# Layer 0 of a two-layer kernel: fourteen products of k with an exponential, made by GpSimd and not by VectorE

## The chip, the cores and the metric

The kernel runs on one core of a Trainium2 chip, as one program with one launch. The metric is the device time of that core in microseconds (us): the median of three runs, and beside it the span of one profiled execution, from its first instruction to its last. In the profile the engines are called PE (TensorE, matrix products and transposes), PEld (its weight loads), DVE (VectorE), ACT (ScalarE), POOL (GpSimd) and SP (SyncE, which issues most of the DMA transfers).

## The reference, cut to what matters

The input x has 4 batches of 512 tokens with 512 channels; fside, called k here, has the same shape and serves as both k and v of the mixing step. Two layers each add to x the result of a mixture of experts, whose input is a token-mixing step (called WKV below). The mixing step of layer 0, for every batch and channel, is:

```python
decay = exp(-exp(w)) * (0.5 + 0.5 * tf)          # one number for each batch and channel
ek = exp(minimum(k, 30));  ekv = ek * k
# two sums with decay over the 512 tokens, forwards (f) and in reverse (b), of ekv and of ek:
#   a = a * decay + ekv[t];   b = b * decay + ek[t]
euk = exp(minimum(u + k, 30))                     # u is the bonus of the channel
num = nf + nb - ekv + euk * k
den = df + db - ek + euk
out = sigmoid(x) * (num / maximum(den, 1e-8)) * (0.8 + 0.2 * tf)
```

`euk` is the exponential that holds the bonus, and `euk * k` is the product that the change is about. `out` is normed, goes to 8 experts (2 for each token) and a shared expert, and is added to x. Layer 1 does the same with its own w and u, and with 32 experts, 6 for each token.

## The kernel before

Channels lie on the 128 partitions and tokens along the free dimension. A unit is one batch and one block of 128 channels, a tile of 128 x 512 in 32 bits; there are NU = 16 of them, numbered n = 4 b + c. Layer 0 works through them in one loop `for n in range(NU)`, followed by routing, a table of slots that is written and read back through DRAM, and the experts (`routed`). Layer 1's WKV (`wkv1`, from line 1043 on) runs on VectorE beside layer 0's experts, and then come layer 1's shared expert and its 32 experts.

The order of instructions on every engine is the order in which the program writes them (a manual schedule for ScalarE, TensorE, VectorE, GpSimd and SyncE). Each engine works through its own queue in that order, and an instruction waits only for the operands it needs and for the buffers it writes.

For one unit the work of layer 0's WKV is spread as follows.

- `turn(n)`: TensorE transposes k, ScalarE copies it to kA (L435, L436).
- `front(n)`: VectorE makes the two arguments of the exponentials (L448, L450), `v[:, 0, :]` and `euk`. There are three buffers of each.
- `front_exps(n)`: ScalarE makes the two exponentials in place (L457, L458).
- `mid(n)`: VectorE multiplies both by k (L465 for the sums, L466 for `eukv`, which has two buffers) and runs `scans`: two scans from the end (L307), a correction of one column (L310), two scans from the front (L312). The scans write over v.
- `sums(n)`: TensorE adds the scans' results and the bonus terms in PSUM, which turns the four sums into den and num (L475, L476; L476 for num reads `eukv`), and ScalarE makes the reciprocal of den as exp(-ln) (L478 to L480).
- `back(n)`: VectorE corrects the reciprocal and forms the output (L487 to L490).

In iteration n the program writes `sums(n - 1)`, then `front(n + 1)` and `front_exps(n + 1)`, then ScalarE and TensorE work for other units and for the shared expert, then `mid(n)`, and then `back(n - 1)`. So the exponentials of a unit are made one iteration ahead of its products, and its products and scans one iteration ahead of its sums. For iterations with b >= 2, GpSimd writes the slots of an earlier batch to the table between the units (`write_slots`, an indirect DMA for each column, L395): three after `mid(n)` in the first two units of a batch and two in the third. In the first units GpSimd also writes zeros to a buffer (L700) and blanks the tables (L292 to L294).

Later, in layer 0's experts, GpSimd makes a product of its own: `hrow` from `upt` and `sgt` (L977), 128 x 256, two operands in SBUF.

Of the kernel before, what the change touches and what calls it, by code (L numbers as in the profile page):

```python
# [14 lines left out]
ALU = mybir.AluOpType  # L15
# [18 lines left out]
def adaln_ffn_kernel(  # L34
# [26 lines left out]
    nc = tc.nc  # L61
# [241 lines left out]
    def scans(l, b, c, v):  # L303

        dec, _, _, inv = (m[:, c, b : b + 1] for m in decay[l])
        for h in range(2):
            nc.vector.tensor_tensor_scan(  # L307
                v[:, h, ::-1], dec.to_broadcast([P, S]), v[:, h, ::-1], 0.0, ALU.mult, ALU.add
            )
        nc.vector.tensor_scalar(v[:, :, 0], v[:, :, 0], inv, None, ALU.mult)  # L310
        for h in range(2):
            nc.vector.tensor_tensor_scan(v[:, h, :], dec.to_broadcast([P, S]), v[:, h, :], 0.0, ALU.mult, ALU.add)  # L312
# [108 lines left out]
    NU = len(units)  # L421
# [38 lines left out]
    def mid(n):  # L460
        b, c = units[n]
        kT = kA[:, c, b * S : (b + 1) * S]
        v, euk = fronts.pop(n)
        eukv = wk.tile([P, S], F32, tag="eukv", name=f"eukv{n}")
        nc.vector.tensor_tensor(v[:, 1, :], v[:, 0, :], kT, ALU.mult)  # L465
        nc.vector.tensor_tensor(eukv, euk, kT, ALU.mult)  # L466
        scans(0, b, c, v)
        mids[n] = (v[:, 0, :], euk), (v[:, 1, :], eukv)

# [224 lines left out]
    for n in range(NU):  # L694
# [12 lines left out]
        if n == 0:  # L707
            mid(0)
# [44 lines left out]
        if n:  # L753
            mid(n)
# [537 lines left out]
    for h in range(NHALF):  # L1292
# [3 lines left out]
        for b in range(NB):  # L1296
            n = f"{h}_{b}"
# [64 lines left out]
```

## Time and profile before

| | before |
|---|---|
| median of three runs | 1505.91 us (1503.96 to 1506.1) |
| the profiled execution | 1506.29 us |
| its span | 1504.5 us |
| PE busy | 1393.8 us, 93% of the span |
| VectorE busy | 696.1 us, 46% |
| ScalarE busy | 397.6 us, 26% |
| GpSimd busy | 572.3 us, 38% |
| L465, L466 (16 of each) | 11.0 us busy in each group, median 684 and 685 ns |
| L307, L312 up to 190 us | 32 of each (two a unit), about 1.2 us one |

Shares of the whole span hide the stages: layer 0's WKV runs from about 10 to 198 us, layer 0's experts with layer 1's WKV from about 235 to 490 us, and TensorE is full in most of what follows. Busy rows in slices are tenths of a slice of 37.6 us. In a timeline each row has a start and a length in us, the engine, the line, the operation with its operands (written tile, arrow, read tiles), and how many equal instructions are merged in it. Where two are merged the length is that of both.

### The profile page before, as it was taken

What the parts mean: (1) busy time and instruction counts of PE and PEld (TensorE: products, weight loads), DVE (VectorE), ACT (ScalarE), POOL (GpSimd) and SP (SyncE); (2) the same over time, 40 slices, a digit from 0 to 9 for tenths busy, and PEclk for the clock granted to TensorE, in tenths of its full rate; (3) what the DMA queues carried; (4) which work ended last, traced back from release to release, by engine and by line L of the source; (5) the groups of instructions that cost most, each with busy time, mean ns of one, the idle gap of its engine ahead of it and who ended that gap; (6) DMA issues with size and microseconds to landing.
All of it is one profiled execution on the core that took longest, in us unless ns stands there. A gap on an engine that the chain in (4) does not pass through costs nothing. (4 is left out here: it accounts for less than half of the span.)

```text
span 1504.5 us, 16067 instructions
## 1 busy us (share of the span) xinstructions
PE 1393.8 (93%) x4927; PEld 823.6 (55%) x4927; DVE 696.1 (46%) x1260; ACT 397.6 (26%) x962; POOL 572.3 (38%) x564
## 2 busy tenths in 40 slices
PE   5788888988878799999999999999999999999997
PEld 3355456766556454444445655555555565555654
DVE  7899958999991259411112222222222222222221
ACT  5667643544443251000001111111111111111110
POOL 1001235665564100545543343434344344333332
PEclk9899999999999999999999999999999999999999
DMA  8121216554454742010136554667446586546442
GB/s 301 67 77 57 78 50 182 89 119 102 94 145 91 241 149 72 1 58 29 48 109 192 132 163 115 165 155 208 105 110 187 143 230 166 139 131 164 109 95 42
DMA packets 118188, 184.71 MB, mean 123 GB/s; under 512 B 19864, under 2 KB 64940, under 8 KB 118040
## 3 DMA queue, kind: packets, MB, share of 16 engines
q1 hardware_dynamic: 82216, 125.28, 24.6%
q0 software_dynamic: 35296, 56.63, 20.4%
q8 instruction: 66, 1.08, 0.3%
q10 hardware_dynamic: 528, 1.05, 0.2%
q14 instruction: 82, 0.67, 0.1%
HBM read 151.02 MB, written 52.64 MB: 135 GB/s over the span
## 5 line engine op out<-in xcount | busy, mean ns | idle before, releaser
L941 PE MATMUL pout<-w,hT 128*128 128x512 f32 (+1 forms) x432 | 201.1, 598 | 1.3 <-DVE hT L934 0.8
L946 POOL DMA_INDIRECT out_dram<-kA,put x52 | 83.0, 1596 | 279.3 <-DVE kA L945 146.2
L900 POOL DMA_INDIRECT acc<-z1d,put x119 | 123.3, 1036 | 123.0 <-PE pza L913 65.2
L982 DVE SCALAR_TENSOR_TENSOR hrow<-pup,tab,sgt 128x352 f32<-128x352 f32 x84 | 49.1, 584 | 249.4 <-issue 128.9
L395 POOL DMA_INDIRECT table<-pay,r1sloti x96 | 95.0, 989 | 172.7 <-ACT sg L1304 111.9
L945 DVE COPY kA<-pout 128x512 f32<-128x512 f32 x84 | 58.1, 692 | 176.0 <-PE pout L941 164.0
L966 PE MATMUL pgate<-w,kA 128*128 128x352 f32 x416 | 132.8, 462 | 6.1 <-PEq L1027 6.0
L970 PE MATMUL pup<-w,kA 128*128 128x352 f32 x416 | 131.6, 459 | 0.0
L941 PEld LDWEIGHTS pout<-w,hT 128*128 128x128 f32 (+1 forms) x432 | 76.8, 192 | 68.1 <-issue 54.1
L981 ACT ACTIVATE sgt<-pgate 128x352 f32<-128x352 f32 x84 | 38.9, 463 | 250.6 <-PE pgate L966 225.8
L966 PEld LDWEIGHTS pgate<-w,kA 128*128 128x128 f32 x416 | 75.3, 190 | 49.9 <-issue 16.6
L913 PEld LDWEIGHTS pza<-ident,acc 128*128 128x128 f32 x584 | 72.0, 141 | 51.9 <-issue 33.1
L970 PEld LDWEIGHTS pup<-w,kA 128*128 128x128 f32 x416 | 77.4, 190 | 39.7 <-issue 0.2
L913 PE MATMUL pza<-ident,acc 128*128 128x128 f32 x584 | 87.1, 274 | 11.3 <-DMA acc<-z0d,put 9.4
L395 POOL DMA_INDIRECT table<-r0pay,r0sloti x32 | 35.0, 1093 | 160.3 <-DVE r0sloti L386 112.1
L923 ACT COPY kA<-pza 128x256 f32<-128x256 f32 x103 | 38.3, 372 | 205.6 <-DVE kA L922 159.8
L900 POOL DMA_INDIRECT acc<-z0d,put x51 | 66.0, 1294 | 58.2 <-ACT zgT L917 40.2
L941 PE MATMUL pout<-zT,hT 128*128 128x512 f32 (+1 forms) x192 | 87.8, 593 | 0.0
L1148 PE MATMUL g<-zT,w 128*128 128x512 f32 (+1 forms) x192 | 86.5, 593 | 0.0
L1148 PE MATMUL u<-zT,w 128*128 128x512 f32 (+1 forms) x192 | 86.3, 592 | 0.0
L1313 PE MATMUL o<-w,kA 128*128 128x512 f32 (+1 forms) x192 | 84.5, 593 | 0.0
L966 PE MATMUL pgate<-zT,kA 128*128 128x352 f32 x256 | 81.3, 460 | 1.9 <-PEq L1027 1.9
(301 smaller groups left out, 2219.0 us busy)
## 6 DMA issues: line engine op xcount, KB each, us to landing
w<-in_L_ffn_w_dram SPq DMA_DIRECT2D x44, 704.0 KB
zT<-in_L_ffn_w_dram SPq DMA_DIRECT2D x20, 704.0 KB
w<-in_L_ffn_w_dram SPq DMA_DIRECT2D x22, 512.0 KB
zT<-in_L_ffn_w_dram SPq DMA_DIRECT2D x10, 512.0 KB
w<-in_L_ffn_w_dram SPq DMA_DIRECT2D x22, 192.0 KB
acc<-in_x_dram SPq DMA_DIRECT2D x4, 1024.0 KB
xa<-acc SPq DMA_DIRECT2D x4, 1024.0 KB
z0d<-zr SPq DMA_DIRECT2D x16, 256.0 KB
```

The lines of the kernel that those rows point to most:

```text
L395: ins = nc.gpsimd.indirect_dma_start(out=table, out_offset=bass.IndirectOffsetOnAxis(ap=sloti[:, t, j : j + 1], axis=0), in_=pay[:, t, j, ...
L900: nc.gpsimd.indirect_dma_start(out=rows(e, s), out_offset=None, in_=zd, in_offset=bass.IndirectOffsetOnAxis(ap=put_at[:, e * NS + s : e * ...
L913: nc.tensor.transpose(pza[which][:, c * P : (c + 1) * P], rows(e, s)[:, c * P : (c + 1) * P], ident)
L941: nc.tensor.matmul(po, hT[:m, j, :], dv[:m, j, :], start=(j == 0), stop=(j == nf - 1))
L945: nc.vector.tensor_copy(row, po)
L946: nc.gpsimd.indirect_dma_start(out=outs(n), out_offset=bass.IndirectOffsetOnAxis(ap=at, axis=0), in_=row, in_offset=None, bounds_check=T - ...
L966: nc.tensor.matmul(pg, zt[:, c, :], gv[:, c, :], start=(c == 0), stop=(c == NC - 1))
L970: nc.tensor.matmul(pu, zt[:, c, :], uv[:, c, :], start=(c == 0), stop=(c == NC - 1))
L981: nc.scalar.activation(sgt, pg, AF.Silu)
L982: nc.vector.scalar_tensor_tensor(hrow, pu, tab[:, col, 1:2], sgt, ALU.mult, ALU.mult)
L1148: nc.tensor.matmul(p[: m + more], wv[:, c, f : f + m + more], zT[:, c, b * S : (b + 1) * S], start=(c == 0), stop=(c == NC - 1),)
L1313: nc.tensor.matmul(po, hid[:m, j, i * P : (i + 1) * P], dv[:m, j, :], start=(j == 0), stop=(j == len(FCH) - 1))
```

## The change

One line of `mid` is changed. For units 1 to 14 the product `eukv = euk * k` is issued to GpSimd, for units 0 and 15 to VectorE as before. Nothing else is edited; on VectorE the scans of a unit now follow L465 directly, and on GpSimd the fourteen products stand among the memsets, the zero and blank writes and the slot writes in the program's order: the product of unit 1 after the three L700, that of unit 2 after both blanked tables, those of units 9 and 10 and of 13 and 14 behind three slot writes each.

```diff
         v, euk = fronts.pop(n)
         eukv = wk.tile([P, S], F32, tag="eukv", name=f"eukv{n}")
         nc.vector.tensor_tensor(v[:, 1, :], v[:, 0, :], kT, ALU.mult)
-        nc.vector.tensor_tensor(eukv, euk, kT, ALU.mult)
+        (nc.gpsimd if 0 < n < NU - 1 else nc.vector).tensor_tensor(eukv, euk, kT, ALU.mult)
         scans(0, b, c, v)
         mids[n] = (v[:, 0, :], euk), (v[:, 1, :], eukv)
```

## The prediction

> **What bounds the kernel now.** First the span in 40 slices of 37.6 us, to see which engine is full where this code runs (the first five slices):
>
> ```profile
> PE   5788888988878799999999999999999999999997
> DVE  7899958999991259411112222222222222222221
> ```
>
> VectorE is at 8 to 9 tenths there, TensorE at 5 to 8. Next the table of windows, which cuts layer 0's sixteen units into stretches (window and its length, then busy us and count for PE, PEld, DVE, ACT and POOL, granted clock, DMA share, GB/s):
>
> ```profile
> 11.00:50.00 39.00, 24.13 (x77) 13.35 (x78) 33.72 (x59) 27.60 (x52) 4.19 (x9) 0.87 0.75 269
> 50.00:95.00 45.00, 38.34 (x134) 22.08 (x135) 43.45 (x73) 26.79 (x50) 0.00 (x0) 0.89 0.29 94
> 95.00:140.00 45.00, 39.96 (x155) 23.18 (x155) 43.25 (x95) 31.65 (x59) 9.41 (x8) 0.99 0.18 65
> 140.00:187.00 47.00, 40.34 (x140) 22.62 (x139) 44.18 (x129) 31.79 (x58) 9.43 (x8) 0.97 0.17 62
> ```
>
> From 50 to 187 us VectorE is busy 130.9 of 137 us, and the rest is the step from one instruction to the next. GpSimd is nearly empty. Third, VectorE's own waits up to 235 us, to see where it is not the bound:
>
> ```profile
> DVE ssq_parts L819 <- ACT sq L791: 5.2, 1, 5.2
> ...
> DVE ratio L274 <- ACT lom L252: 3.5, 1, 3.5
> ...
> DVE zT L490 <- ACT zT L498: 1.0, 1, 1.0
> ```
>
> In the timeline the 3.45 us wait ends at 44.36 us and the 0.97 us wait at 28.81; the 5.2 us wait lies behind the last unit, at 201 us. So up to 44.4 us ScalarE sets the pace (it runs without a gap from 36.6 to 44.3), and from 44.4 to 198 us VectorE does. After that a chain of logits, routing, table writes (to 229 us) and the first gather (235 us) hangs on VectorE's last unit, and TensorE fills nearly all the rest. What VectorE wins or loses between 44.4 and 198 us therefore moves everything behind it, one for one; the chain of waits at the end of the span shows only the last expert and says nothing of this stage.
>
> **What is removed.** Fourteen of the sixteen L466 products leave VectorE. One unit as it runs now (start, length, engine, line):
>
> ```profile
> 54.31 0.68 DVE L465 TENSOR_TENSOR v<-v,kA 128x512 f32<-128x512 f32 x1
> 54.91 0.68 DVE L466 TENSOR_TENSOR eukv<-euk,kA 128x512 f32<-128x512 f32 x1
> ...
> 55.52 2.33 DVE L307 TENSOR_TENSOR_SCAN v<-dec,v 128x512 f32<-128x512 f32 x2
> ...
> 56.20 0.61 ACT L458 ACTIVATE euk<-euk 128x512 f32<-128x512 f32 x1
> ```
>
> One product lasts 0.68 us but holds its queue from 54.91 to 55.52, 0.61 us, since the next instruction starts under its tail. Units 1 and 2 (L466 at 20.17 and 30.76 us) lie before 44.36 us: their time only lengthens the 3.45 us wait, so they win nothing. Units 3 to 14 win 12 x 0.605 = 7.3 us.
>
> **What is added, and when.** GpSimd has nothing queued that holds a product up for long, so it starts one as soon as ScalarE has made that unit's euk. The ACT line above is already the euk of unit 5, one unit ahead: it ends at 56.81 us, inside unit 4's scans. The ends of L458 for units 6, 7, 8, 11 and 12 fall likewise (65.74, 77.05, 87.77, 126.23, 135.74 us), beside the scan pairs of the unit before; that of unit 4 (44.22) meets L465 of unit 3. Units 9 and 13 sit behind three table writes each (to about 113 and 161 us), and fall on their own first scans; units 10 and 14 sit behind three more and fall on the four instructions of `back`. The product is wanted late (TensorE's L476 of unit 13 is at 169.69 us, 7 us after that product would end), and its buffer is free in time, so I cost lateness at nothing: the cover is the 6 (unit 2) to 16 us (unit 5) between a product's end and its L476. Table writes behind a product move 1.3 us; the table is read only at 231 us. Product 3 (at 36.7 us) and those before it may cost up to the 3.45 us wait for free. That leaves products 4 to 14, eleven.
>
> **What one costs.** The trace has the same operation at half the size: layer 0's experts multiply hrow on GpSimd while VectorE runs layer 1's scans. Its row, and two places where it meets VectorE:
>
> ```profile
> L977 POOL TENSOR_TENSOR hrow<-upt,sgt x35: 726/742/1737, 247.4 to 490.4; 128x256 f32<-128x256 f32 x35
> ```
>
> ```profile
> 336.09 1.56 DVE L1054 TENSOR_TENSOR zT<-zT,kA 128x512 f32<-128x512 f32 x1
> ...
> 336.36 0.73 POOL L977 TENSOR_TENSOR hrow<-upt,sgt 128x256 f32<-128x256 f32 x1
> ```
>
> ```profile
> 316.01 3.38 DVE L307 TENSOR_TENSOR_SCAN v<-dec,v 128x512 f32<-128x512 f32 x2
> 316.71 1.60 POOL L977 TENSOR_TENSOR hrow<-upt,sgt 128x256 f32<-128x256 f32 x1
> ```
>
> L1054 takes 0.69 us undisturbed, here 1.56; two scans take 2.33, here 3.38; and the GpSimd product itself stretches from 0.73 to 1.60. The two engines take turns. I went through all thirty products between 247 and 453 us. The nine that lie under the one-input reciprocal (L1057) leave it at 3.35 us. The other twenty-one cost VectorE 0.29 to 1.05 us each, 12.5 us together, 0.60 on average; the twelve among them at scan pairs average 0.58. A single-input L1051 doubles as well (0.96 for 0.48).
>
> The duration at 512 columns has no row. Bounds from L977: 0.73 us, if all of it were fixed, and 1.48, if none were. The Trainium skill, GPSIMD Engine Reference, section Performance versus the Vector engine, gives 4497 ns for such an operation on 2048 columns; a line through that and the row's 742 at 256 has 2.1 ns a column, so an estimate of 742 + 256 x 2.1 = 1278 ns. The row measures the small end; I take 1.28 and keep 1.48. The 0.54 us that are added hold VectorE in full where it is held at all, so one product costs 0.60 + 0.54 = 1.14 us. Bounds: 0.29 (the added length hides) to 1.05 + 0.74 = 1.79.
>
> A rule to weigh against that: the same skill's page SBUF — State Buffer, section SBUF: two separate sides, says that GpSimd shares one pair of ports with VectorE, that an instruction keeps it to its end, and that only a VectorE instruction with two SBUF inputs or in a two-port mode needs it. By the rule alone each product takes its whole 1.28 us: 11 x 1.28 - 7.3 = +6.8 us. The rows charge less, since an instruction's start-up runs under the other's tail (0.29 at scan ends for a 0.73 us product): 11 x 1.14 - 7.3 = 12.5 - 7.3 = **+5.2 us**. The rows decide.
>
> Against the profiled execution (1506.29 us, its span 1504.5 and 1.8 around it) that gives 1511.5 us; it stands 0.4 above the median of 1505.91, so I predict **1511.1 us**.
>
> **The rivals.** (1) *GpSimd truly runs beside the scans.* The removed time comes through: 1505.9 - 7.3 = 1498.6 us. For it: VectorE is the bound and GpSimd empty. Against: the stretched L307 and L977 above. It would be faster by a measurable amount only if a product cost under (7.3 - 3.0)/11 = 0.39 us; three of the twenty-one did, at half the size. This is the one on the other side. (2) *The loss about cancels the gain:* products 10 and 14 meet L487 and L489, which read one operand from PSUM and may pass freely, and some added length hides. With 0.4 to 0.9 us a product, 4.4 to 9.9 - 7.3: 1503.0 to 1508.5 us. (3) *The dear collision is the rule:* three of six products that start in the first scan of a pair cost 1.0 or so; if all do, 11 x (1.0 + 0.54) - 7.3 = +9.7, or 1515.6 us; at 1.48 us long, 1517.8. (4) *GpSimd's queue is late* and L476 waits: it needs over 6 us of delay behind table writes that take 1.0 to 1.9 us each, three at a time; no time of its own. That nothing is moved is excluded: the built program has fourteen L466 on GpSimd and two on VectorE.
>
> **How the numbers follow.** About 0.2% (3 us) can be told from no change. Forecast 0.60 (1509 to 1514), rival 3 0.12, rival 2 0.19, rival 1 0.08, the rest 0.01. Slower by over 3 us: 0.60 + 0.12 = 0.72. Within: 0.19 + 0.01 = 0.20. Faster: 0.08. The range leaves out rival 1, the bottom of rival 2 and the rare top: 1503.5 to 1517.5.
>
> **What would show it.** VectorE's L466 count falls from 16 to 2, and a POOL row for L466 x14 appears, above 1.28 us on average because it waits. L307 and L312 before 190 us show lengths of 1.7 us or more where all are about 1.2 now. The time from L465 of unit 3 to L465 of unit 15 (44.66 and 186.66 us now, 142.0 us) grows by about 5 us, and later stages keep their length. If that distance shrinks, the scans are not held, and I am wrong; if it grows and the total doesn't, the stage was not what moves the rest; if POOL's L466 last 1.28 us with scans untouched, rival 1 holds.

## The result and the profile after

The changed kernel takes 1512.64 us (median of 9 runs, 1511.32 to 1514.87) against 1506.10 us (9 runs, 1503.96 to 1510.47). The ratio is 1.0042, with a 95% interval of 1.0032 to 1.0052: slower by 6.3 us, between 4.8 and 7.8. The forecast was 1511.1 us, slower by 5.2.

The profiled execution took 1514.87 us, with a span of 1513.1 us. It is the slowest of the nine, so below its stages are compared and not its total.

First the group of the moved products, with the shortest, median and longest duration in ns:

```profile
L466 POOL TENSOR_TENSOR eukv<-euk,kA x14: 1270/1500/2131, 21.1 to 170.1; 128x512 f32<-128x512 f32 x14
...
L466 DVE TENSOR_TENSOR eukv<-euk,kA x2: 685/685/685, 11.4 to 192.9; 128x512 f32<-128x512 f32 x2
```

Fourteen of sixteen have moved. One lasts 1.27 us where it doesn't wait, and half of them last 1.50 us or more. Next the table of windows, in the stretches that were shown of before:

```profile
50.00:95.00 45.00, 37.93 (x132) 21.50 (x133) 43.52 (x61) 25.96 (x49) 6.96 (x4) 0.89 0.29 94
95.00:140.00 45.00, 40.13 (x148) 22.61 (x146) 43.06 (x94) 29.29 (x56) 14.24 (x12) 0.96 0.18 65
140.00:187.00 47.00, 40.46 (x143) 23.16 (x142) 44.73 (x100) 31.07 (x58) 12.95 (x11) 0.96 0.17 62
```

VectorE (third pair) is busy 131.3 of 137 us, as before (130.9), but it gets less far: 255 instructions in that time and not 297, and the moved products are only eleven of the difference. It is "busy" with instructions that wait inside themselves, and for neither an operand nor a buffer. A wait of this kind shows in no list of waits. It shows in the length of single instructions, as here in unit 4 (timeline of the changed kernel):

```profile
54.45 0.68 DVE L465 TENSOR_TENSOR v<-v,kA 128x512 f32<-128x512 f32 x1
...
55.16 2.34 DVE L307 TENSOR_TENSOR_SCAN v<-dec,v 128x512 f32<-128x512 f32 x2
...
56.68 1.88 POOL L466 TENSOR_TENSOR eukv<-euk,kA 128x512 f32<-128x512 f32 x1 [11.56 <-ACT euk L458]
...
57.54 1.04 DVE L310 TENSOR_SCALAR v<-v,inv 128x2 f32<-128x2 f32 x1
```

The product of unit 5 starts as soon as its euk is there, inside the second scan of unit 4. It waits for that scan, runs, and L310, a correction of one column that takes 0.23 us, takes 1.04. The same unit before, with the two scans from the front behind it:

```profile
57.88 0.23 DVE L310 TENSOR_SCALAR v<-v,inv 128x2 f32<-128x2 f32 x1
58.15 2.34 DVE L312 TENSOR_TENSOR_SCAN v<-dec,v 128x512 f32<-128x512 f32 x2
```

The products of units 7 and 9 in the changed kernel:

```profile
77.74 1.27 POOL L466 TENSOR_TENSOR eukv<-euk,kA 128x512 f32<-128x512 f32 x1 [9.18 <-ACT euk L458]
...
77.86 3.35 DVE L312 TENSOR_TENSOR_SCAN v<-dec,v 128x512 f32<-128x512 f32 x2
...
113.36 2.39 DVE L465 TENSOR_TENSOR v<-v,kA 128x512 f32<-128x512 f32 x1
...
113.91 1.27 POOL L466 TENSOR_TENSOR eukv<-euk,kA 128x512 f32<-128x512 f32 x1
```

The pair of scans takes 3.35 us where it took 2.34, and L465 takes 2.39 where it took 0.68. What products 4 to 14 cost VectorE, each read off the stretched instruction against its length before:

| product of unit | VectorE instruction held | us lost |
|---|---|---|
| 4 | L274 (1.24 for 0.17) | 1.07 |
| 5, 6, 8, 12 | L310 (1.04 or 1.05 for 0.23) | 0.81 to 0.82 |
| 7, 10, 11, 14 | the pair L312 (3.35 to 3.37 for 2.34) | 1.02 to 1.03 |
| 9, 13 | L465 (2.39 and 2.40 for 0.68) | 1.71 |

Together they cost 11.85 us, 1.08 on average. VectorE's waits before 245 us have changed in two places that matter:

```profile
DVE t L487 <- ACT r L480: 1.2, 1, 1.2
DVE ratio L274 <- ACT lom L252: 1.0, 1, 1.0
```

The wait at L274, 3.45 us before, has taken up what the first three products cost. The wait at L487 of the last unit was 0.49 us before. The start of a unit's L465 against before tells the rest: unit 3 +0.61 us, unit 9 +1.15, unit 10 +3.44, unit 13 +3.84, unit 14 +6.16, unit 15 +5.69. The table that was read back is converted at 240.2 us, before at 233.7: **+6.5 us**, about what the medians differ by. Its rows, before and after (the start stands behind the durations in ns):

```profile
L850 POOL CAST put<-tab x1: 960/960/960, 233.7 to 233.7; 128x128 int32<-128x128 f32 x1
```

```profile
L850 POOL CAST put<-tab x1: 1206/1206/1206, 240.2 to 240.2; 128x128 int32<-128x128 f32 x1
```

### The profile page after: what moved, and what is told of

Read it like the earlier page. It is cut to its first block, busy times and chain, and to the rows that moved or that the text cites. A ratio compares the mean times of both kernels' runs of the same rounds, so it can differ in the third digit from the quotient of the medians.

```text
span 1513.1 us, 16077 instructions
## 1 busy us (share of the span) xinstructions
PE 1399.0 (92%) x4927; PEld 827.1 (55%) x4927; DVE 702.2 (46%) x1246; ACT 397.2 (26%) x962; POOL 590.0 (39%) x578
## 3 DMA queue, kind: packets, MB, share of 16 engines
q8 instruction: 66, 1.08, 0.3%
q10 hardware_dynamic: 528, 1.05, 0.2%
## 5 line engine op out<-in xcount | busy, mean ns | idle before, releaser
L312 DVE TENSOR_TENSOR_SCAN v<-dec,v 128x512 f32<-128x512 f32 x64 | 80.5, 1300 | 1.1
```

## The experiments

A total of a single run is a weak measure here. Layer 0's experts, from the table to layer 1's first sigmoid, took 287.7 us in the profiled execution of before and 286.2 to 292.4 us in those of kernels that do the same work there. The start of unit 3, where VectorE takes over the pace from ScalarE, varies too: three runs below have it 1.5 to 1.8 us earlier than before, one of them with more work on VectorE. So each run is read first by how the start of a unit's L465 (or the same product under a shifted line number) moves against before from unit 3 to unit 15. By this measure the change stands at +5.08 us. The totals, against runs of the kernel before on the same chip, stand beside it.

**The product left out.**

```diff
-        nc.vector.tensor_tensor(eukv, euk, kT, ALU.mult)
+        if not 0 < n < NU - 1:
+            nc.vector.tensor_tensor(eukv, euk, kT, ALU.mult)
...
-        mids[n] = (v[:, 0, :], euk), (v[:, 1, :], eukv)
+        mids[n] = (v[:, 0, :], euk), (v[:, 1, :], euk if 0 < n < NU - 1 else eukv)
```

> Leaves out the product of units 1 to 14 on every engine (their sums read euk in its place, so num is not the reference's there). Theory (the stage is VectorE's and moves all behind it, and each product gone gives back 0.50 us, as the units without a collision in the changed kernel's trace show): 12 x 0.50 = 6.0 us less, about 1500 us, no L307 or L312 above 1.25 us before 200 us. Rival (another engine takes over as the bound as soon as VectorE is relieved): less than 2 us gained, with new idle time on VectorE between 45 and 190 us.

In the trace every undisturbed unit gains 0.47 to 0.50 us, and from unit 3 to unit 15 the start moves by -5.0 us (from -1.83 to -6.84); the table is converted at 226.9 us, 6.8 earlier. The total is 1508.61 us all the same, ratio 1.0025 (1.0017 to 1.0033). The reason lies in the experiment: with other numbers in num the router chooses other experts, and layer 0 gets 37 tiles of 128 slots where it had 35 (the count of hrow products in the two profiles). So the run shows the size of the gain and that it is passed on as far as the table, and its total says nothing. One wait of 0.72 us appeared, VectorE for ScalarE's sum of squares.

**The product on both engines.** GpSimd writes the buffer first, VectorE after it.

```diff
+        if 0 < n < NU - 1:
+            nc.gpsimd.tensor_tensor(eukv, euk, kT, ALU.mult)
         nc.vector.tensor_tensor(eukv, euk, kT, ALU.mult)
```

> VectorE keeps all sixteen products, and GpSimd makes those of units 1 to 14 too, into the same buffer and ahead of VectorE. Theory (the two engines take turns): the collisions alone, eleven at 1.08 us on average, 11.9 us, so about 1518 us. Rival (the change loses by handing TensorE the product later, or by GpSimd's queue): VectorE hands over as before, so within 2 us of 1506.

1524.99 us, ratio 1.0123 (1.0107 to 1.0139). From unit 3 to unit 15 the start grows from +4.79 to +17.45 us, 12.7 us for ten collisions (that of product 4 falls ahead of unit 3's L465). The 4.8 us before that come for the most part from VectorE's waits for GpSimd's writes of units 1 and 2 (2.3 and 2.9 us), which my design brought in and which I had overlooked. TensorE gets the product from VectorE at its old place, so late handover isn't what costs: the collisions are. In units 9 and 13 they cost 3.5 us each, where the change lost 2.3 net of its gain: L465 again takes 2.39, and the next unit's product now meets the first scan of L312 at its start, which takes 3.04 us for 1.22.

**The product beside `back`.**

```diff
+        if on_pool:
+            hold(nc.gpsimd.tensor_tensor(eukv, euk, kT, ALU.mult), "scan")
```

Here `marks["scan"]` is the last scan of the unit, and `on_pool` is true for units 1 to 14.

> As the change, but GpSimd's product waits for the last scan of its own unit, so that it runs beside the four instructions of back. Theory, if only an instruction with two operands in SBUF has to take turns: L487, which reads den from PSUM, passes, L488 waits about 0.65 us; 12 x (0.65 - 0.50) = 2 us, about 1508 us. If every VectorE instruction has to take turns, each product costs its 1.27 us less little: 12 x (1.2 - 0.5) = 8 us, about 1514 us. Rival (late handover): the product is 3 to 5 us later than in the change, so slower than the change, above 1513 us.

```profile
68.80 0.67 DVE L493 SCALAR_TENSOR_TENSOR t<-den,r 128x512 f32<-128x512 f32 x1
...
69.06 1.28 POOL L473 TENSOR_TENSOR eukv<-euk,kA 128x512 f32<-128x512 f32 x1 [8.58 <-DVE v L312]
...
69.50 1.38 DVE L494 SCALAR_TENSOR_TENSOR t<-t,r 128x512 f32<-128x512 f32 x1
```

L493 (L487 before), which reads den from PSUM, keeps its 0.67 us under the running product. L494, with both operands in SBUF, takes 1.38 for 0.69. Such a unit loses 0.69 and gains 0.49, +0.20 us, and six units show just that. Five show +0.47 to +0.53; they have small routing instructions between the scans and back, and one of these is held (a cast of 32 columns takes 1.14 us for 0.18). From unit 3 to unit 15 the start grows by 3.82 us, where the change has 5.08, with a later handover: in the stage the place decides. The total does not show it: 1512.68 us, ratio 1.0038 (1.0024 to 1.0052), about that of the change and more than the stage accounts for (the table is at +3.3 us). In the profiled execution 1.9 us more came in layer 0's experts, which is inside the spread given above; what holds the median up is open.

**Two halves.** The first 256 columns wait for the last scan, the others for L488.

```diff
+            hold(nc.gpsimd.tensor_tensor(eukv[:, : S // 2], euk[:, : S // 2], kT[:, : S // 2], ALU.mult), "scan")
...
+            hold(nc.gpsimd.tensor_tensor(eukv[:, S // 2 :], euk[:, S // 2 :], kT[:, S // 2 :], ALU.mult), "t")
```

> As the run before, but in two halves of 256 columns, the first behind the last scan (beside L487), the second behind L488 (beside L489); both of these read one operand from PSUM. Theory: each half lasts 0.73 us and overhangs by about 0.15 us into L488 and L490: 12 x (0.30 - 0.50) = 2.4 us less, about 1504 us. Rival (late handover): later still than whole, above 1513 us.

Five units gain 0.34 to 0.42 us, but units 10, 11, 14 and 15 start 1.17, 0.74, 2.05 and 0.59 us later against the unit before them. L500 is the second half. In the program's order it stood behind the slot writes of its iteration (three, of 1.0 to 1.3 us each), and that had two effects. It fell on L469 and L307 (L465 and L307 before) of the next unit:

```profile
109.30 1.22 DVE L469 TENSOR_TENSOR v<-v,kA 128x512 f32<-128x512 f32 x1
...
109.86 1.23 POOL L500 TENSOR_TENSOR eukv<-euk,kA 128x256 f32<-128x256 f32 x1
...
110.55 2.74 DVE L307 TENSOR_TENSOR_SCAN v<-dec,v 128x512 f32<-128x512 f32 x2
```

Here that is 0.53 and 0.41 us; over the four units such collisions stretch VectorE's instructions by about 3.2 us. And TensorE waited for it (between 100 and 130 us):

```profile
PE num L485 <- POOL eukv L500: 2.7, 2, 2.0
```

Behind TensorE's waits, in its queue, stand the transposes for ScalarE's sum of squares, for which VectorE then waited 0.49 and 1.15 us. So lateness, a rival that I gave no time, does occur once the product is made late enough, but collisions are the larger part of this loss. From unit 3 to unit 15 the start grows by 2.58 us (from -1.37 to +1.21); total 1510.37 us, ratio 1.0026 (1.0015 to 1.0036).

**Two halves, ahead of the slot writes.**

```diff
-        if b >= 2 and c < 3:
-            if c == 0:
-                route_slots(b - 2)
-            write_slots(b - 2, 3 if c < 2 else 2)
+        if b >= 2 and c == 0:
+            route_slots(b - 2)
...
         if n:
             back(n - 1)
+        if b >= 2 and c < 3:
+            write_slots(b - 2, 3 if c < 2 else 2)
```

> As the halves, but GpSimd's slot writes of an iteration stand behind the second half in its queue and not ahead of it. Theory (each half's place decides): all twelve units from 3 to 14 gain 0.35 us as the undisturbed ones of the run before did, 4.2 us, and unit 15 starts 4 to 6 us earlier than before (the early wait shrinks too); about 1501 us. Rival (in the run before, something other than the writes ahead of the second half held units 9, 10, 13 and 14): those four keep their extra 0.6 to 2.1 us and the stage ends no earlier than before.

```profile
90.29 0.67 DVE L496 SCALAR_TENSOR_TENSOR t<-den,r 128x512 f32<-128x512 f32 x1
...
90.54 0.73 POOL L475 TENSOR_TENSOR eukv<-euk,kA 128x256 f32<-128x256 f32 x1 [7.16 <-DVE v L312]
...
90.99 0.83 DVE L497 SCALAR_TENSOR_TENSOR t<-t,r 128x512 f32<-128x512 f32 x1
...
91.90 0.73 POOL L500 TENSOR_TENSOR eukv<-euk,kA 128x256 f32<-128x256 f32 x1 [0.63 <-DVE t L497]
...
91.92 0.69 DVE L501 TENSOR_TENSOR t<-num,t 128x512 f32<-128x512 f32 x1
```

Both halves now lie under the PSUM readers, and only L497 is longer, by 0.14 us. The late units are gone (10 and 14: -0.35 and -0.29). In this execution unit 6 lost 1.07 us: VectorE waited 1.33 us at 73 us for ScalarE's sum of squares, behind matmuls that ran at half their speed from 63 to 66 us (a pair in 1.91 us that takes 1.02; the granted clock was 0.59 from 62 to 67 us, before 0.84). Unit 15 starts at -1.36 us (-0.98 against unit 3), not at the -4 to -6 expected, since the five units with routing behind the scans gain next to nothing (-0.08 to +0.16). The total is 1505.69 us, ratio 0.9999 (0.9991 to 1.0007). With the same fourteen products on GpSimd, the loss of the change is gone, and no gain that can be measured has taken its place. What moving the slot writes does by itself was not tried.

**VectorE makes the product twice,** GpSimd none.

```diff
         nc.vector.tensor_tensor(eukv, euk, kT, ALU.mult)
+        if 0 < n < NU - 1:
+            nc.vector.tensor_tensor(eukv, euk, kT, ALU.mult)
```

> VectorE makes the product of units 1 to 14 twice, GpSimd none. Theory (VectorE's time from unit 3 on moves all that follows, one for one): 12 x 0.61 = 7.3 us, about 1513 us, and the table of slots is read 7 us later. Rival (part of the stage's shift is absorbed later, so that a gain of some us here could not be seen at the end either): the table read is 7 us later, but the total under 4 us.

Units 4 to 15 each add 0.70 to 0.73 us (once 1.02): the second product into the same buffer starts 0.72 us behind the first, not 0.61. From unit 3 to unit 15 that is 8.95 us (from -1.52 to +7.43); the table is converted 7.5 us later, and the total is 1515.32 us, ratio 1.0062 (1.0049 to 1.0075), 9.3 us (7.4 to 11.3). A delay of VectorE in this stage is passed on whole.

**What GpSimd must do to collide: a copy and a fill in the product's place.** In both VectorE keeps its products.

```diff
+        if 0 < n < NU - 1:
+            nc.gpsimd.tensor_copy(eukv, euk)          # one run
+            nc.gpsimd.memset(eukv, 1.0)               # the other run
         nc.vector.tensor_tensor(eukv, euk, kT, ALU.mult)
```

> VectorE keeps all sixteen products, and GpSimd copies euk into the same buffer ahead of it, for units 1 to 14: one operand read from SBUF and not two. If it is GpSimd's reading of SBUF that VectorE's scans must take turns with: scan pairs or L310 beside a copy are longer by about the copy's own length. If it takes two operands on GpSimd's side: all scan pairs stay at 2.33 us.

> VectorE keeps all sixteen products, and GpSimd fills the same buffer with a constant ahead of it, for units 1 to 14: it writes SBUF and reads nothing. If only a GpSimd instruction that reads SBUF has to take turns with two-operand VectorE instructions: scan pairs beside a fill stay at 2.33 us. If writing is enough: they are longer by 0.5 us or more.

The copy, then the fill, each beside a pair of scans:

```profile
56.66 0.73 POOL L467 COPY eukv<-euk 128x512 f32<-128x512 f32 x1 [9.34 <-ACT euk L458]
...
56.83 2.74 DVE L307 TENSOR_TENSOR_SCAN v<-dec,v 128x512 f32<-128x512 f32 x2
```

```profile
75.05 2.33 DVE L307 TENSOR_TENSOR_SCAN v<-dec,v 128x512 f32<-128x512 f32 x2
...
75.59 0.52 POOL L467 MEMSET eukv<- 128x512 f32 x1 [10.20 <-PE num L478]
```

A copy (0.61 us alone) makes the pair 0.36 to 0.41 us longer. A fill leaves it at 2.33, at every one of the places where it meets scans. Here a GpSimd instruction that only writes SBUF doesn't collide with the scans, and one that also reads it does. The units' starts agree: from unit 3 to 15 +3.95 us with the copy, +0.90 with the fill, all of the latter at units 9 and 13, where VectorE waited for the fill itself behind the slot writes. It waited for the copy there too (0.50 us each), so about 3 of the 3.95 us are collisions. The totals, one run each, are 1517.04 and 1510.01 us; in the copy's trace layer 0's experts alone took 4.7 us more than before.

**The first three only.**

```diff
-        nc.vector.tensor_tensor(eukv, euk, kT, ALU.mult)
+        (nc.gpsimd if 0 < n < 4 else nc.vector).tensor_tensor(eukv, euk, kT, ALU.mult)
```

> Only the products of units 1, 2 and 3 go to GpSimd. Theory (up to 44 us ScalarE sets the pace, so what these three take from VectorE only shortens its 3.45 us wait at L274): the wait at L274 falls to about 1 us, L465 of unit 3 starts within 0.2 us of before, L465 of unit 4 0.5 us earlier (the product of unit 3 is gone there), and that 0.5 us is still there at unit 15; total within 2 us of before. Rival (these products delay the stage as the others do): L465 of unit 3 starts 2 us or more later.

The wait at L274 falls to 1.02 us, unit 3 starts at -0.15 us and unit 4 at -0.62. At unit 15 it is +0.19: VectorE waited at two places (0.19 and 0.52 us) for ScalarE's sum of squares, and the head start was lost. The total is 1508.16 us beside one run of before at 1508.52.

**Half the columns in the change's place.**

```diff
+            nc.gpsimd.tensor_tensor(eukv[:, lo], euk[:, lo], kT[:, lo], ALU.mult)
+            nc.vector.tensor_tensor(eukv[:, hi], euk[:, hi], kT[:, hi], ALU.mult)
```

Here `lo` and `hi` are the two halves of the 512 columns, in units 1 to 14.

> For units 1 to 14 GpSimd makes the first 256 columns of the product where the change puts the whole, and VectorE makes the other 256 at the old place. Theory (a collision costs a start-up part and the length of the GpSimd instruction, 0.53 us for 256 columns): 1.08 - 0.53 = 0.55 us for each of eleven, 6.1 us, less 12 x 0.26 = 3.1 us for the shorter product on VectorE; unit 15 starts about 3 us later than before. Rival (a collision has a price of its own, whatever the size): 11 x 1.08 - 3.1, unit 15 about 9 us later.

```profile
53.86 2.82 DVE L307 TENSOR_TENSOR_SCAN v<-dec,v 128x512 f32<-128x512 f32 x2
...
53.96 1.63 POOL L468 TENSOR_TENSOR eukv<-euk,kA 128x256 f32<-128x256 f32 x1 [8.24 <-ACT euk L458]
```

A pair of scans costs 0.48 us more here, where the whole product cost 1.02: the 0.54 us that were added for 256 more columns hold VectorE in full. From unit 3 to 15 the start grows by 2.51 us (from -1.61 to +0.90), near the 3 expected and far from the rival's 9; against before alone, as the expectation has it, unit 15 is only 0.90 us later. One run, 1507.53 us beside 1508.52 of before.

## Why the prediction was right, point by point

- **What bounds the stage.** Right. Doubling the product moved unit 15 by 8.95 us against unit 3 and the end by 9.3; leaving it out moved unit 15 by -5.0 us against unit 3. The distance from unit 3 to unit 15, named beforehand as the sign to look for, grew by 5.08 us in the change, where about 5 was forecast.
- **What is removed.** 12 x 0.605 = 7.3 us was too much; it is 12 x 0.49 = 5.9. I took the step from one product to the next instruction, 0.61 us. With L466 gone, the first scan follows L465 and starts 0.71 us behind it (54.45 to 55.16 above), so 0.1 us a unit comes back. That the scan waits for L465's tail, since both touch v, would explain it; it was not tried alone.
- **When the products run.** Right for those made one unit ahead, and for 9 and 13 behind the slot writes, though these two met L465 of their own unit and not its first scans. Wrong for 10 and 14, which I put beside `back`: they met L312 of the unit before, at 1.02 us each. The sum had charged all eleven alike, so this error did not show in it. The rest of that idea, that PSUM readers pass freely, was shown by the run behind the scans.
- **What one costs.** 1.14 us was forecast, 1.08 measured, and the duration alone was 1.27 us for the estimate of 1.28. The mean hides a spread from 0.81 to 1.71: the dearest are the two that meet L465 at its start, which I had not priced apart.
- **The sum.** 11.85 - 5.9 = 5.95 us, where the forecast said 12.5 - 7.3 = 5.2; unit 15 starts 5.69 us later. Both terms were too large, by 0.65 and 1.4 us, and in the difference part of this cancelled, which is luck. To the 5.69 come 0.75 us at the last unit, where L487 waited for r: TensorE's sixteen matmuls ahead of it took 6.17 us, before 5.41, at a granted clock of 0.60 and 0.68. A shift of 6.5 us at the table follows. Whether the change causes these 0.75 us is open: the same wait is 0.97 us in the run with the first three only, whose unit 15 is 0.19 us late, and 0.50 in both runs with halves.
- **The rule on the shared ports** would have given +6.8 us and the rows gave +5.2; 6.3 lies between. The rule had the kind of instruction right (the fill passes, the reader of PSUM passes, the two-operand instructions don't), and the rows had the price. Instructions with one tensor operand are held as well where they are a tensor_scalar or a cast; the rule allows for that with its two-port mode, and no run here shows whether they are in it.
- **The rivals.** True overlap is excluded by the stretched L307, L310, L312 and L465. The cancelling case did not occur, as no product found a free place. The dear collision was not the rule: only products 9 and 13 cost more than the 1.54 us that it was given. Lateness did not occur in the change, where TensorE's list of waits from 40 to 200 us has none for eukv, and did, as the smaller part of the loss, in the first version with halves.

## What to carry to other kernels

Before an elementwise product is given to an idle GpSimd, look at what VectorE runs at that moment: where it has two operands in SBUF, the two engines took turns here, and most of the slower engine's duration (1.08 of 1.27 us) was paid in place of the faster one's. The price is found by comparing single VectorE lengths where GpSimd is active, since it shows in no wait and in no busy share. If the product must move, place it by a dependency under VectorE instructions that read an operand from PSUM, and look at what stands ahead of it in GpSimd's own queue. One operand is not enough to be free: a reciprocal passed (3.35 us with and without), but L310, a tensor_scalar of two elements, and a cast of 32 columns were held.

## What the runs showed of the hardware that was not expected

- A GpSimd fill of 128 x 512 (0.52 us) ran beside scans at no cost to them, while a copy (0.61 us) cost 0.36 to 0.41 us.
- A two-operand VectorE instruction that is caught at its start loses more than GpSimd's instruction lasts: L465 lost 1.71 us to a product of 1.27, and L465 had been issued 0.55 us before the product was recorded to start. A scan caught like this lost 1.82 us. The slot write that runs on GpSimd just ahead of the product does not hold L465 by itself: before, an L465 under one took 0.69 us. What does is open.
- L310, which handles two elements a partition and has one tensor operand, is held as well, 0.81 us.
- In six of the runs VectorE met waits of 0.2 to 1.3 us for ScalarE's sum of squares, which it doesn't meet before. In five of the six it was ahead of its old time there, and in the sixth, with the product made twice, it was 2.8 us behind. So a part of a gain in this stage can be lost again; with the product left out it was 0.8 of 5.8 us.
